# A larger VectorE share, half as many interleaved sets, and waits joined to operations, in a kernel that writes all products of the columns of a batch

## The chip, the cores and the metric

The kernel runs on one core of a Trainium2 chip. The time is the device time of that core in microseconds (us): the median of three runs for the kernel before. The profile is one execution recorded by the hardware profiler, whose span is a little shorter than the device time (1270.1 us against 1272.28 us for the same run).

Engines in the profile: DVE is VectorE, ACT is ScalarE, POOL is GpSimd, SP is SyncE, which here only issues transfers. A trailing q (DVEq, SPq) means the sequencer in front of an engine, which handles waits, counts and issues. Data leaves the core by 16 DMA engines that work side by side.

## The reference

```python
def reference(r_inputs):                       # r_inputs: (4096, 256), float32
    dot = jnp.einsum('bi,bj->bij', inputs, inputs)
    iu, ju = jnp.triu_indices(256)
    return dot[:, iu, ju]                      # (4096, 32896), float32
```

Each of the 4096 rows of 256 numbers becomes the 32,896 products of its upper triangle: x0\*x0, x0\*x1, ... x0\*x255, x1\*x1, and so on. The "triangle row" i of the output holds x_i times x_i ... x_255 and is 256 - i long. The input is 4.19 MB and the output 538.97 MB, so the kernel mostly writes.

## The kernel before

The 4096 batch rows lie as 128 partitions with 32 rows each. Two rows per partition (REPEAT = 2) make a *round*: 16 rounds in all. In each round the 32,896 output columns are cut into three *pieces* of 10,944, 10,976 and 10,976 columns, so there are 48 pieces. Two buffers (*places*) hold a piece each, in turn: while one is being written out by DMA, the other is filled.

A piece is filled by two engines. The front of its list of triangle rows goes to ScalarE (one operation for each triangle row and each of the two batch rows, a copy with a per-partition scale), the rest goes to VectorE (an elementwise multiplication which does both batch rows at once). `split` hands rows to ScalarE until what is left for VectorE fits a budget per element:

```python
BUDGETS = [0.85, 0.85, 0.85]
SETS = 4
PASS = 6        # pieces in one turn of the loop
AHEAD = 2
...
def vector_time(block):
    return sum(68 + 1.046 * REPEAT * n * m for (*_, n), m in vector_ops(block))

def split(block, budget):
    scalar, k = 0.0, 0
    while k < len(block):
        scalar += REPEAT * (184 + 0.837 * block[k][3])
        if vector_time(block[k:]) <= budget or scalar > vector_time(block[k + 1 :]):
            break
        k += 1
    return k                       # block[:k] to ScalarE, block[k:] to VectorE
```

One VectorE operation may take two neighbouring triangle rows (m = 2). The second row is one element shorter than the first, so such an operation writes one element too many, which falls on the first element of the next row, and the operation that writes that next row must come later. To leave time between the two, `interleave` cuts VectorE's list into SETS stretches and takes operations from each stretch in turn. An operation whose predecessor in its own stretch was a double one has to wait for a count on VectorE's own semaphore `v_own`:

```python
    def vector(h, pieces, ahead):
        done = 0
        for p in pieces:
            ...                    # every third piece: copy the new round's rows to xv
            if not ahead:
                take(nc.vector, free[p % PLACES], 16)   # wait until the place is written out
                nc.vector.sem_inc(go, 1)                # let ScalarE begin
            for _, _, _, block, lo in blocks(p, ahead):
                order = interleave(block)
                counted, waits = {len(order) - 1}, {}
                for k, (*_, before) in enumerate(order):
                    if before is not None and before > max(waits.values(), default=-1):
                        waits[k] = max(before, k - 2)
                        counted.add(waits[k])
                ...
                    if k in waits:
                        ins._wait_ge(v_own, number[waits[k]])
                    if k in counted:
                        ins.then_inc(v_own, 1)
                ...
                nc.vector.wait_ge(v_own, done).then_inc(v_done, 1)
```

`take` is a wait that also sets the count back. ScalarE's first operation of a piece waits for `go`. SyncE waits for `v_done` and `a_done` of a piece and then issues its transfer, which raises `free` of that place by 16 when all of it has landed:

```python
                if not ahead:
                    turns += 1
                    todo[0]._wait_ge(go, turns)                 # ScalarE
...
                take(nc.sync, v_done, 1)                        # SyncE
                take(nc.sync, a_done, 1)
                nc.sync.dma_start(...).then_inc(free[p % PLACES] if len(parts) == 1 else head, 16)
```

The first two pieces are filled before the loop (the first of them in five parts, so that transfers can begin early). The loop then has 8 turns; a turn fills four pieces (2, 3, 4, 5 of a group of six) and then, except in the last turn, pieces 0 and 1 of the next group:

```python
        with nc.Fori(0, passes, ...) as h:
            pieces_of(h, range(AHEAD, PASS), False)
            with engine.If(h < passes - 1):
                pieces_of(nc.s_assert_within(h + 1, 0, passes - 1), range(AHEAD), False)
```

Of the kernel before, what the change touches and what calls it, by code (L numbers as in the profile page):

```python
# [14 lines left out]
REPEAT = 2  # L15
PIECES = 3
PLACES = 2
SETS = 4
PASS = 6
AHEAD = 2  # L20


BUDGETS = [0.85, 0.85, 0.85]
FIRST = [512, 1536, 3584, 6400]


# [5 lines left out]
def runs(d: int, lo: int, hi: int) -> list:  # L32


    found, at = [], 0
    for i in range(d):
        a, b = max(at, lo), min(at + d - i, hi)
        if a < b:
            found.append((i, i + a - at, a, b - a))
        at += d - i  # L40
    return found


def vector_ops(block: list) -> list:

    ops, k = [], 0
    while k < len(block):  # L50
        i, j, at, n = block[k]
        m = 2 if k + 2 < len(block) and i == j else 1
        ops.append((block[k], m))
        k += m
    return ops


def interleave(block: list) -> list:


    sets, k = [], 0
    for left in range(SETS, 0, -1):
        share = -(-len(vector_ops(block[k:])) // left)
        end = k
        while end < len(block) and len(vector_ops(block[k : end + 1])) <= share:
            end += 1
        if left == 1:
            end = len(block)
        sets.append(vector_ops(block[k:end]))
        k = end  # L70
    order, last = [], {}
    for step in range(max(map(len, sets))):
        for s, ops in enumerate(sets):
            if step < len(ops):
                order.append((*ops[step], last.get(s)))
                last[s] = len(order) - 1 if ops[step][1] == 2 else None
    return order
# [6 lines left out]
def split(block: list, budget: float) -> int:  # L84
# [8 lines that stand above are left out]
    return k  # L93


def window(ap: bass.AP, free: list) -> bass.AP:
    return bass.AP(ap.tensor, ap.offset, [list(ap.ap[0]), *free])
# [3 lines left out]
def kernel(  # L101
# [14 lines left out]
    nc = tc.nc  # L116
# [4 lines left out]
    passes = groups // rounds  # L121
# [17 lines left out]
    def semaphore(name: str):  # L139
        return ctx.enter_context(nc.semaphore(name))  # L140

    free = [semaphore(f"free{k}") for k in range(PLACES)]
    head, v_done, a_done, go = (semaphore(s) for s in ("head", "v_done", "a_done", "go"))
# [3 lines left out]
    def take(engine, sem, value: int):  # L147
        engine.wait_ge(sem, value).then_inc(sem, -value)  # L148

    v_own, a_own = semaphore("v_own"), semaphore("a_own")  # L150

    def x_of(h, q: int) -> bass.AP:
        return xt[:, bass.ds(h, 1), q * each : (q + 1) * each].rearrange("p o d -> p (o d)")

    def blocks(p: int, ahead: bool):

        lo, hi = spans[p % PIECES]
        cuts = [lo, *(FIRST if ahead and p == 0 else []), hi]
        for a, b in zip(cuts, cuts[1:]):
            block = runs(d, a, b)  # L160
            k = split(block, 0.0 if ahead else BUDGETS[p % PIECES] * REPEAT * (b - a))
            yield a - lo, b - lo, block[:k], block[k:], lo

    def vector(h, pieces: range, ahead: bool):
        done = 0
        for p in pieces:
            place = places[p % PLACES]
            if p % PIECES == 0:
                ins = nc.vector.tensor_copy(xv[:, :each], x_of(h, p // PIECES))  # L169
                if done:  # L170
                    ins._wait_ge(v_own, done)
                ins.then_inc(v_own, 1)
                done += 1
                nc.vector.wait_ge(v_own, done)
            if not ahead:
                take(nc.vector, free[p % PLACES], 16)
                nc.vector.sem_inc(go, 1)  # L177
            for _, _, _, block, lo in blocks(p, ahead):
                order = interleave(block)

                counted, waits = {len(order) - 1}, {}
                for k, (*_, before) in enumerate(order):
                    if before is not None and before > max(waits.values(), default=-1):
                        waits[k] = max(before, k - 2)
                        counted.add(waits[k])
                number = {k: done + 1 + c for c, k in enumerate(sorted(counted))}
                for k, ((i, j, at, length), m, _) in enumerate(order):
                    at -= lo
                    ins = nc.vector.tensor_tensor(  # L189
                        place[:, :, at : at + m * length],  # L190
                        window(xv[:, j:], [[d, REPEAT], [1, m], [1, length]]),
                        window(xv[:, i:], [[d, REPEAT], [1, m], [0, length]]),
                        ALU.mult,
                    )
                    if k in waits:
                        ins._wait_ge(v_own, number[waits[k]])
                    if k in counted:
                        ins.then_inc(v_own, 1)
                done += len(counted)
                nc.vector.wait_ge(v_own, done).then_inc(v_done, 1)  # L200
        nc.vector.sem_inc(v_own, -done)  # L201

    def scalar(h, pieces: range, ahead: bool):
        done = turns = 0
# [42 lines left out]
                )  # L247

    def all_pieces(engine, pieces_of):
        pieces_of(0, range(AHEAD), True)  # L250
        if engine is not nc.sync:
            for sem in loaded[1:]:
                engine.wait_ge(sem, 16)
        kind = engine.engine
        with nc.Fori(
            0,
            passes,
            engines=OrderedEngineSet([kind]),
            head_slot={kind: 0} if engine is not nc.sync else {},
        ) as h:  # L260
            pieces_of(h, range(AHEAD, PASS), False)
            with engine.If(h < passes - 1):
                pieces_of(nc.s_assert_within(h + 1, 0, passes - 1), range(AHEAD), False)

    for (lo, hi), sem in zip(zip(loads, loads[1:]), loaded):
        nc.sync.dma_start(xt.rearrange("p h d -> p (h d)")[:, lo:hi], x_in[:, lo:hi]).then_inc(sem, 16)
# [6 lines left out]
    for engine, pieces_of in ((nc.vector, vector), (nc.scalar, scalar), (nc.sync, sync)):  # L273
        all_pieces(engine, pieces_of)
    for k in range(PLACES):
        take(nc.sync, free[k], 16)
    for sem in loaded:
        take(nc.sync, sem, 16)

# [26 lines left out]
```

## Time and profile before

| | before |
|---|---|
| median of 3 runs | 1272.26 us (1272.22 to 1272.28) |
| span of the profile | 1270.1 us |
| DVE busy | 896.2 us, 71%, 1733 instructions |
| ACT busy | 632.1 us, 50%, 1897 instructions |
| written to and read from HBM | 538.97 MB and 4.19 MB, 428 GB/s over the span |
| ACT idle before its piece, until DVE's sequencer raised `go` | 593.2 us, 46 times |
| DVE idle before its piece, until the place was free | 328.6 us, 46 times |

How to read it: "busy" counts the time in which an engine carries out an operation. An engine that is idle costs nothing unless something that sets the end waits for it. L189 is the line of VectorE's multiplication, L213 that of ScalarE's scaled copy, L148 the line of `take`, L177 the line that raises `go`, L245 the issue of a piece's transfer. "Landing" is the moment at which a transfer's last count has arrived.

### The profile page before, as it was taken

Reading aid. Unit: us, or ns where it says so; the run is one execution under the profiler, and the core shown is the slowest. Engines: PE = TensorE matmul, PEld = TensorE weight load, DVE = VectorE, ACT = ScalarE, POOL = GpSimd, SP = SyncE. Lnnn points to the kernel's source line nnn. Section 1 sums busy time; section 2 is a strip of 40 time slices with the busy share of each in tenths; the row PEclk is TensorE's granted clock in tenths of the full one; section 3 lists DMA queues with packets and bytes.
Section 4 is the critical chain, followed back from the end, with each engine's and each line's share of the span. In section 5 each row is a group of like instructions: output and inputs, shape, how many; then the busy total and the mean of one; then the engine's idle time right before and its main releaser. Section 6 shows DMA issues by size and latency. Waiting matters only on the chain. (4 is left out here: it accounts for less than half of the span.)

```text
span 1270.1 us, 4343 instructions
## 1 busy us (share of the span) xinstructions
DVE 896.2 (71%) x1733; ACT 632.1 (50%) x1897; POOL 0.2 (0%) x4
## 2 busy tenths in 40 slices
DVE  8867776777667776677757776677766777577760
ACT  8635635455364543645437453374534735257350
POOL 0000000000000000000000000000000000000000
DMA  9999999999999999999999999999999999999997
GB/s 380 437 440 426 437 440 422 441 422 440 422 441 421 440 423 439 430 432 439 424 437 424 439 423 440 422 440 425 437 428 433 422 442 420 441 421 441 421 420 336
DMA packets 14582, 543.22 MB, mean 428 GB/s; under 512 B 880, under 2 KB 880, under 8 KB 1520
## 3 DMA queue, kind: packets, MB, share of 16 engines
q1 hardware_dynamic: 14576, 543.17, 99.4%
q14 instruction: 6, 0.05, 0.0%
HBM read 4.19 MB, written 538.97 MB: 428 GB/s over the span
## 5 line engine op out<-in xcount | busy, mean ns | idle before, releaser
L189 DVE TENSOR_TENSOR o<-xv 128x752 f32<-128x752 f32 (+62 forms) x1716 | 889.3, 605 | 329.3 <-DVEq L148 328.6
L213 ACT ACTIVATE o<-xa 128x253 f32<-128x253 f32 (+58 forms) x1880 | 620.8, 423 | 593.4 <-DVEq L177 593.2
L169 DVE COPY xv<-x 128x512 f32 (+1 forms) x16 | 6.8, 427 | 9.0 <-DVEq L201 4.2
L208 ACT ACTIVATE xa<-x 128x512 f32 (+1 forms) x16 | 10.1, 630 | 5.6 <-ACTq L235 3.9
L208 ACT ACT_TABLE_LOAD x1 | 1.3, 1283 | 4.0 <-DMA x<-in_r_inputs_dram 4.0
L267 DVE MEMSET xv<- 128x1 f32 x1 | 0.1, 59 | 1.0 <-SPq L137 1.0
L293 POOL MEMSET const-bfloat16-1.0<- 128x1 bf16 x1 | 0.1, 102 | 0.0
L293 POOL MEMSET const-uint8-127<- 128x1 uint8 x1 | 0.1, 102 | 0.0
L293 POOL MEMSET const-float32-1.0<- 128x1 f32 x1 | 0.1, 99 | 0.0
L293 POOL MEMSET const-float32-0.0<- 128x1 f32 x1 | 0.1, 98 | 0.2 <-issue 0.2
## 6 DMA issues: line engine op xcount, KB each, us to landing
out_dram<-o SPq DMA_DIRECT2D x32, 10976.0 KB, 33.0
out_dram<-o SPq DMA_DIRECT2D x15, 10944.0 KB, 32.9
out_dram<-o SPq DMA_DIRECT2D x1, 4544.0 KB, 18.7
out_dram<-o SPq DMA_DIRECT2D x1, 2816.0 KB, 14.1
x<-in_r_inputs_dram SPq DMA_DIRECT2D x1, 2048.0 KB, 12.3
out_dram<-o SPq DMA_DIRECT2D x1, 2048.0 KB, 11.6
x<-in_r_inputs_dram SPq DMA_DIRECT2D x1, 1792.0 KB, 6.9
out_dram<-o SPq DMA_DIRECT2D x1, 1024.0 KB, 10.0
```

The source lines that it names most:

```text
L169: ins = nc.vector.tensor_copy(xv[:, :each], x_of(h, p // PIECES))
L189: ins = nc.vector.tensor_tensor(place[:, :, at : at + m * length], window(xv[:, j:], [[d, REPEAT], [1, m], [1, length]]), window(xv[:, i:] ...
L208: nc.scalar.activation(xa, x_of(h, p // PIECES), AF.Copy).then_inc(a_own, 1)
L213: nc.scalar.activation(place[:, r, at - lo : at - lo + length], xa[:, r * d + j : r * d + j + length], AF.Copy, scale=xa[:, r * d + i : r ...
L267: nc.vector.memset(xv[:, each:], 0.0)
L293: nc = _bacc.Bacc("TRN2", target_bir_lowering=False, num_devices=1)
```

## The change

The change does four things.

1. The budgets rise from 0.85 to 1.0, 1.0 and 0.95 ns per element of the three pieces of a round, so VectorE takes more triangle rows and ScalarE fewer: 74 ScalarE operations in a round in place of 116 (10, 16 and 48 in the three pieces, in place of 22, 32 and 62).
2. VectorE's list is interleaved from two stretches in place of four. It then has fewer operations for the same rows, because fewer pairs are cut at the borders of stretches, and each waiting operation comes two places behind the one that it waits for.
3. Waits and counts that stood as instructions of their own are joined to operations: the end of a piece raises `v_done` directly where `v_own` need not be told, and the count on `v_own` runs on from the four pieces into the next two.
4. A place's `free` count is no longer set back at each use. It runs to 16, 32, 48 over the three uses of a place in a group of six pieces. At the first two uses the wait for it raises `go` itself; at the third use (pieces 0 and 1 of the next group) the wait sets `free` back, and `go` is raised by a VectorE operation: the first of the piece that does not already raise `v_own`.

The purpose is to take instructions and ScalarE work out of the filling of a piece.

```diff
-SETS = 4
+SETS = 2
-BUDGETS = [0.85, 0.85, 0.85]
+BUDGETS = [1.0, 1.0, 0.95]
...
+    uses = PASS // PLACES
+    def use(p: int) -> int:
+        return (p - AHEAD) % PASS // PLACES + 1
...
             if not ahead:
-                take(nc.vector, free[p % PLACES], 16)
-                nc.vector.sem_inc(go, 1)
+                if use(p) < uses:
+                    nc.vector.wait_ge(free[p % PLACES], 16 * use(p)).then_inc(go, 1)
+                else:
+                    take(nc.vector, free[p % PLACES], 16 * uses)
...
-                counted, waits = {len(order) - 1}, {}
+                own = (p + 1) % PIECES == 0 or p == pieces[-1]
+                counted, waits = {len(order) - 1} if own else set(), {}
...
+                lets_go = -1
+                if not ahead and use(p) == uses:
+                    lets_go = next(k for k in range(len(order)) if k not in counted)
...
                     if k in counted:
                         ins.then_inc(v_own, 1)
+                    if k == lets_go:
+                        ins.then_inc(go, 1)
                 done += len(counted)
-                nc.vector.wait_ge(v_own, done).then_inc(v_done, 1)
-        nc.vector.sem_inc(v_own, -done)
+                if own:
+                    nc.vector.wait_ge(v_own, done).then_inc(v_done, 1)
+                else:
+                    ins.then_inc(v_done, 1)
+        return done
```

(The rest of the diff carries `done` through the loop and sets the counts back at its end.)

## The prediction

> **What bounds the kernel now.** I read the page's DMA part first, because the kernel mostly writes.
>
> ```profile
> DMA packets 14582, 543.22 MB, mean 428 GB/s; under 512 B 880, under 2 KB 880, under 8 KB 1520
> q1 hardware_dynamic: 14576, 543.17, 99.4%
> ```
>
> The transfer queue occupies the 16 DMA engines for 99.4% of the span, so the engines that fill the places are hidden at present. Whether they stay hidden depends on how early each transfer is issued, so next I took the timeline of three pieces in mid-run (columns: start, length, engine, line, operation, count, idle time before).
>
> ```profile
> 380.38 8.80 ACT L213 ACTIVATE o<-xa 128x256 f32<-128x256 f32 x22 [7.12 <-DVEq L177]
> 380.43 18.55 DVE L189 TENSOR_TENSOR o<-xv 128x980 f32<-128x980 f32 x20 [6.85 <-DVEq L148]
> 406.43 11.11 ACT L213 ACTIVATE o<-xa 128x7 f32<-128x7 f32 x32 [17.25 <-DVEq L177]
> 406.49 18.46 DVE L189 TENSOR_TENSOR o<-xv 128x776 f32<-128x776 f32 x26 [7.50 <-DVEq L148]
> 432.42 18.39 ACT L213 ACTIVATE o<-xa 128x98 f32<-128x98 f32 x62 [14.88 <-DVEq L177]
> 432.47 18.83 DVE L189 TENSOR_TENSOR o<-xv 128x468 f32<-128x468 f32 x61 [7.52 <-DVEq L148]
> ```
>
> A piece comes every 26.1 us (380.43 to 458.86, the next piece 0, is 78.43 for three). VectorE needs 18.5 to 18.8 us of it and then waits about 7 us for the other place. Its wait ends with a landing, so every piece starts at one.
>
> Last, the end of the run, in stretches (columns: window, length, busy DVE, ACT and POOL, clock, DMA share, GB/s).
>
> ```profile
> 1235.90:1236.40 0.50, 0.00 (x0) 0.00 (x0) 0.00 (x0) 1.00 0.00 0
> 1236.40:1236.90 0.50, 0.00 (x0) 0.00 (x0) 0.00 (x0) 1.00 2.29 966
> ...
> 1263.40:1265.00 1.60, 0.00 (x0) 0.00 (x0) 0.00 (x0) 1.00 0.06 27
> 1265.00:1266.60 1.60, 0.00 (x0) 0.00 (x0) 0.00 (x0) 1.00 0.06 27
> 1266.60:1268.20 1.60, 0.00 (x0) 0.00 (x0) 0.00 (x0) 1.00 0.06 27
> 1268.30:1270.00 1.70, 0.00 (x0) 0.00 (x0) 0.00 (x0) 1.00 0.00 0
> ```
>
> Two things are seen. The last transfer is issued at 1235.92 and the first packets after it start about 0.9 us later; the packet records put them at 1236.8 to 1237.0, so I use 0.95 us. And at the end one DMA engine alone works on (a share of 0.06, one sixteenth) for 5.3 us after the fifteen others are done. That slowest engine sets every landing and the end. In the landing records its lag grows from about 0.3 us at 328 us to 5 us at 1000 us and then stays, because the other fifteen then run dry for some tenths of a microsecond at each issue. The quantity that matters is therefore whether the *slowest* engine ever runs dry.
>
> **What the Trainium skill says.** "DMA: Bandwidth & Descriptors", section "Where 436 GB/s comes from", puts the ceiling of the 16 ports at 435 GB/s and says that the HBM side, about 358, binds such transfers. Here three pieces (33.69 MB) in 78.43 us are 430 GB/s, so the trace agrees with the first figure and not with the second. The same page, section "Latency and other measured facts", says that two of the engines, 7 and 15, are usually slower; the trace shows one slow engine, but not its number. "Perfetto Trace Analysis", section "DVE / Act Engine Instruction (TENSOR_ADD, Activation, etc)", says that an operation's count goes out only when all its bytes are acknowledged, at the end that the profile reports. The trace agrees: the count instruction that waits for a piece's last VectorE operation starts 39 ns after its end. Point three below rests on it. "VectorE: DVE Perf Modes", section "The DRAIN you can't avoid", measured that a count on every operation costs nothing extra; the trace agrees so far, as counted and waiting operations keep the same spacing as others.
>
> **The change part by part.** VectorE first. The kernel's own formula, 68 ns an operation and 1.046 ns an element, gives 18.51, 18.42 and 18.71 us for the 20, 26 and 61 operations before, against 18.55, 18.46 and 18.83 in the timeline, so I trust it. After the change the lists are 22 operations with 2 x 9694 elements (1.50 + 20.28 = 21.78 us), 29 with 2 x 9553 (1.97 + 19.99 = 21.96) and 63 with 2 x 7811 (4.28 + 16.34 = 20.63). In the third piece short operations (the last have a formula time of 72 to 150 ns) stand between an operation and the one it waits for, and I add up to 0.6 us there. So VectorE takes 21.8, 22.0 and about 21.1 us.
>
> How much would be harmless? For the slowest engine count from the landing that frees a place: 0.25 us until VectorE starts (landing at 380.18 in the records, start 380.43), the filling D, 0.4 us until the issue (372.91 to 373.30), 0.95 us until packets flow. The engine runs dry 26.1 us after that landing, less the 0.47 us which lie between a transfer's last packet and its landing (1268.30 and 1268.77): 25.65 us. So D may reach 24.05 us. All three VectorE times are below it. Of the four pieces 2 to 5 of a group nothing reaches the end; that part is worth 0 us. Joined counts save 0.1 to 0.2 us a piece, hidden likewise.
>
> Second, ScalarE's own time falls to 4.09 us (piece 0: its first ten operations, from 380.38) and 5.50 us (piece 1: its first sixteen). These are the same triangle rows as before, so the profile has them measured:
>
> ```profile
> 380.38 4.09 ACT L213 ACTIVATE o<-xa 128x256 f32<-128x256 f32 x10 [7.12 <-DVEq L177]
> ...
> 406.43 5.50 ACT L213 ACTIVATE o<-xa 128x7 f32<-128x7 f32 x16 [17.25 <-DVEq L177]
> ```
>
> Third, and this decides: at the third use of a place (pieces 0 and 1 of the next group) `go` is raised by the first VectorE operation that does not already raise `v_own`. With two stretches, each operation from the third on waits for the one two places before it, so almost all are counted. Worked through the lists: in piece 0, of 22 operations, numbers 0 to 19 are counted, so number 20 raises `go`; in piece 1, of 29, numbers 0 to 25 and the last are counted, so number 26 raises it. ScalarE, which before started with VectorE, starts there when VectorE has nearly finished.
>
> Piece 0: operation 20 starts 21.78 - 0.55 - 0.49 = 20.73 us in and takes 0.63 us (462 elements; the 128x460 operation before took 631 ns): 21.36. With 0.05 for the count and 4.09 for ScalarE, D is 25.5 us. Piece 1: 20.97 + 0.53 (352 elements) = 21.50, and with 0.05 and 5.50 it is 27.05 us.
>
> From landing to flowing packets: piece 0 takes 0.16 (no separate `go` any more) + 25.5 + 0.26 (ScalarE's count goes straight to SyncE) + 0.95 = 26.87 us against 25.65, so the slowest engine stands still for 1.2 us. Piece 1 takes 0.13 + 27.05 + 0.26 + 0.95 = 28.4 us. Its place came free with the transfer before piece 0's, and piece 0's transfer now ends 1.2 us late, so the allowance is 25.65 + 1.2 = 26.85 and it adds 1.5 us. The next piece has room again (its landing moved as well). That is 2.7 us a turn, in the seven turns that have the two pieces: 7 x 2.7 = 19 us. 1272.3 + 19 = 1291 us.
>
> The start and the end add nothing that I can see: the pieces before the loop keep their split, and the last turn has no third use.
>
> **Rivals.** (a) *Nothing moves*, 1272 us: the queue is 99.4% busy and VectorE's longer filling is inside its 7 us wait. This is right for pieces 2 to 5, and would hold for all if ScalarE's release came early. Against it stands the list of counted operations. (b) *VectorE becomes the bound*: if a wait on the operation two places back held each one by 0.1 us, D would grow by 2 to 3 us in pieces 0 and 1 and 6 us in piece 2; the stall would be 5 to 8 us a turn for pieces 0 and 1, and piece 2 would stall too, for 1310 us or more. Against it: 19 such waits in the third piece before left its total at 0.1 us over the formula. (c) *The slow DMA engine catches up.* All sixteen restart together in each turn. If its slowness, about 0.13 us a piece against the others, came from working while they rest, up to 5 us come back: 1286 us. (d) *Restarts cost more* than 0.95 us when all engines are dry: half a microsecond more, 14 times, makes 1298 us.
>
> **Range and chances.** The sum rests on two differences of about 1.2 and 1.5 us, each from terms good to 0.3 us, taken seven times: 4 us either way; (c) takes some off and (d) adds some. I choose 1284 to 1297 us. The 2% line is 1297.7 us, so slower by over 2% needs 3.6 us a turn in place of 2.7: a chance of 0.08. Faster by 2% would need less data to write: 0.01.
>
> **What would show it.** Right: in pieces 0 and 1 of six, ScalarE starts about 21.4 us after VectorE and waits for a VectorE operation, not for its sequencer; those issues come about 1.2 and 1.5 us after the slow engine ran dry; landings are 27.3 and 27.6 us apart there and 26.1 elsewhere. VectorE's pieces take 21.8, 22.0 and 21.1 us. Wrong: ScalarE starting with VectorE in all pieces (then rival a); VectorE's pieces over 24 us (rival b); stalls much over or under 2.7 us a turn.

## The result, and the profile after

| | before | after |
|---|---|---|
| median of four runs | 1272.26 us (1272.22 to 1272.28) | 1291.14 us (1291.06 to 1291.27) |
| ratio after to before | | 1.0148, 95% interval 1.0133 to 1.0163 |
| span of the profile | 1270.1 us | 1289.0 us |
| instructions in the profile | 4343 | 3720 |
| DVE busy | 896.2 us | 1030.1 us |
| ACT busy | 632.1 us | 413.1 us |
| DMA queue's share of 16 engines' span | 99.4% | 98.0% |

The change makes the kernel 18.9 us slower, 1.5%. The prediction was 1291 us, in a range of 1284 to 1297.

The page's DMA part after, to be held against the same two lines of before:

```profile
DMA packets 14582, 543.22 MB, mean 421 GB/s; under 512 B 880, under 2 KB 880, under 8 KB 1520
q1 hardware_dynamic: 14576, 543.17, 98.0%
```

Packets and bytes are the same. The share times the span is 0.994 x 1270.1 = 1262 us before and 0.980 x 1289.0 = 1263 us after, so the transfers themselves take as long as they did; what is new is time in which the queue has nothing to move.

The timeline of one turn of the loop shows where (start, length, engine, line, operation, count, idle time before and who ended it). The lines are pieces 0, 1 and 2, and then piece 0 of the next round, which is one of those with an early release:

```profile
465.00 21.80 DVE L202 TENSOR_TENSOR o<-xv 128x1004 f32<-128x1004 f32 x22 [4.57 <-DVEq L148]
486.34 4.08 ACT L231 ACTIVATE o<-xa 128x256 f32<-128x256 f32 x10 [32.13 <-DVE o L202]
491.05 21.98 DVE L202 TENSOR_TENSOR o<-xv 128x808 f32<-128x808 f32 x29 [4.26 <-DVEq L148]
512.52 19.95 ACT L231 ACTIVATE o<-xa 128x7 f32<-128x7 f32 x64 [22.10 <-DVE o L202]
518.15 20.89 DVE L202 TENSOR_TENSOR o<-xv 128x496 f32<-128x496 f32 x63 [5.11 <-DMA out_dram<-o]
...
545.92 4.08 ACT L231 ACTIVATE o<-xa 128x256 f32<-128x256 f32 x10 [12.62 <-DVEq L183]
545.98 21.80 DVE L202 TENSOR_TENSOR o<-xv 128x1004 f32<-128x1004 f32 x22 [6.27 <-DMA out_dram<-o]
```

In the first piece ScalarE starts 21.34 us after VectorE (486.34 and 465.00), in the second 21.47 us after it, each time released by a VectorE operation (`<-DVE o L202`). In the last two lines, an early release, the two engines start together. The x64 of the fourth line is the 16 operations of piece 1 and then the 48 of piece 2, without a gap.

The waits of the whole run (engine and line, waited for whom: us in total, times, longest) give the count: 14 late releases, two in each of seven turns.

```profile
ACT o L231 <- DVEq L183: 446.1, 26, 22.0
ACT o L231 <- DVE o L202: 379.6, 14, 32.2
```

Last, the DMA engines around those two pieces' transfers (window, length, busy DVE, ACT, POOL, clock, DMA share, GB/s):

```profile
490.40:491.50 1.10, 0.45 (x1) 0.02 (x1) 0.00 (x0) 1.00 0.00 0
491.50:492.00 0.50, 0.50 (x2) 0.00 (x0) 0.00 (x0) 1.00 3.29 1401
...
518.00:519.00 1.00, 0.85 (x2) 0.92 (x5) 0.00 (x0) 1.00 0.00 0
519.00:519.50 0.50, 0.50 (x2) 0.50 (x3) 0.00 (x0) 1.00 3.30 1405
```

These windows book a packet where it starts, which is why a share can exceed 1 and why a share of 0.00 alone does not show that the engines rest. The packet records give each packet's length as well: from 490.42 to 491.57 us and from 517.67 to 519.14 us no DMA engine has a packet. The whole run has 14 such gaps, two in each of seven turns, 18.3 us together; the loss is 18.9 us. In the kernel before, the packet records of the loop have no such gap: at least one engine, the slowest, always has work.

### The profile page after: what moved, and what is told of

Same layout as the page of the kernel before. It is cut to its first block, busy times and chain, and to the rows that moved or that the text cites. A ratio compares the mean times of both kernels' runs of the same rounds, so it can differ in the third digit from the quotient of the medians.

```text
span 1289.0 us, 3720 instructions
## 1 busy us (share of the span) xinstructions
DVE 1030.1 (80%) x1835; ACT 413.1 (32%) x1253; POOL 0.2 (0%) x4
## 5 line engine op out<-in xcount | busy, mean ns | idle before, releaser
L202 DVE TENSOR_TENSOR o<-xv 128x124 f32<-128x124 f32 (+61 forms) x1818 | 1023.2, 647 | 217.0 <-DMA out_dram<-o 148.0
L231 ACT ACTIVATE o<-xa 128x253 f32<-128x253 f32 (+38 forms) x1236 | 401.7, 416 | 826.4 <-DVEq L183 446.1
```

Of the source, the lines that this page charges most:

```text
L202: ins = nc.vector.tensor_tensor(place[:, :, at : at + m * length], window(xv[:, j:], [[d, REPEAT], [1, m], [1, length]]), window(xv[:, i:] ...
L231: nc.scalar.activation(place[:, r, at - lo : at - lo + length], xa[:, r * d + j : r * d + j + length], AF.Copy, scale=xa[:, r * d + i : r ...
```

## The experiments

The theory is that of the prediction: the late release of ScalarE makes two fillings a turn too long, and a filling costs nothing until it is so long that the slowest DMA engine stands still. (A *filling* here is the time from VectorE's first operation of a piece to the last operation of either engine.) The rivals are that VectorE's longer filling costs, that its waits on nearly every operation do, or that the two engines' working one after the other costs in proportion.

### The release early again, all else changed

```diff
+LATE = ()
...
                 else:
                     take(nc.vector, free[p % PLACES], 16 * uses)
+                    if p not in LATE:
+                        nc.vector.sem_inc(go, 1)
...
-                if not ahead and use(p) == uses:
+                if not ahead and use(p) == uses and p in LATE:
                     lets_go = next(k for k in range(len(order)) if k not in counted)
```

> Only the release of ScalarE at the third use of a place is put back to where it was before: ahead of VectorE's first operation. VectorE's share, the two stretches and all joined waits stay as in the changed kernel. Theory (the late release alone makes DMA engines run dry): the whole 18.9 us come back, 1272.3 us, within 1 us. Rival (VectorE's longer filling of 21 to 22 us costs, or waiting on nearly every operation does): 1291 us, or something between.

Measured: 1271.80 us, ratio 0.9996 (0.9988 to 1.0005). The whole loss is gone. The timeline of the same two pieces:

```profile
458.80 4.08 ACT L234 ACTIVATE o<-xa 128x256 f32<-128x256 f32 x10 [10.83 <-DVEq L188]
458.86 21.80 DVE L205 TENSOR_TENSOR o<-xv 128x1004 f32<-128x1004 f32 x22 [4.67 <-DVEq L149]
484.85 5.50 ACT L234 ACTIVATE o<-xa 128x7 f32<-128x7 f32 x16 [21.97 <-DVEq L188]
484.90 21.98 DVE L205 TENSOR_TENSOR o<-xv 128x808 f32<-128x808 f32 x29 [4.25 <-DVEq L149]
```

VectorE works as long as in the changed kernel (21.80 and 21.98 us), ScalarE begins with it, and a piece comes every 26 us again. VectorE's share, its two stretches and its waits cost nothing here.

The landing records show why longer fillings are free at first. The last transfer's slowest engine ends at 1268.66 us, against 1268.77 in the kernel before, but the fifteen others end by 1266.24 and not by 1263.32. With fillings of 22 us in place of 18.5 to 18.8 us, the fifteen end 3 us later, and the time does not move: the packet records still have no gap common to all engines, so the slowest one, which sets the end, still never stops.

### Four stretches, and the rule of the release untouched

```diff
-SETS = 2
+SETS = 4
```

> The changed kernel with four stretches in place of two, and nothing else. The rule that picks the releasing operation is untouched, but with four stretches the first operation of pieces 0 and 1 does not raise the count on VectorE's semaphore, so it now raises ScalarE's release: 1.1 to 1.3 us into the piece and not 21.4. Theory: 1272.3 us, within 1 us. Rival (joining the release to an operation costs in itself): 1291 us.

Measured: 1270.76 us, ratio 0.9988 (0.9981 to 0.9995). One constant, which does not mention the release, takes the loss away, because with four stretches the first operation of a piece is free to raise it:

```profile
458.37 21.86 DVE L202 TENSOR_TENSOR o<-xv 128x1004 f32<-128x1004 f32 x23 [4.60 <-DVEq L148]
459.61 4.08 ACT L231 ACTIVATE o<-xa 128x256 f32<-128x256 f32 x10 [11.96 <-DVE o L202]
```

ScalarE is again released by a VectorE operation, but 1.24 us into the piece. So joining the release to an operation costs nothing in itself; what costs is which operation it is. It is also the fastest kernel of this study, 0.12% ahead of the kernel before. I had expected 1272.3 us. Of the 1.5 us, 1.1 are spread over the whole run: from the landing at 172 us to the last one, the same 42 pieces take 1095.4 us here and 1096.6 us before (1096.4 with two stretches and an early release, the run above), so the slowest DMA engine itself is faster by about 0.03 us a piece. Why is open.

### A smaller VectorE share, with the late release

```diff
-BUDGETS = [1.0, 1.0, 0.95]
+BUDGETS = [0.85, 0.85, 0.85]
```

> The changed kernel with VectorE's budgets back at 0.85, so VectorE works less (18.5 us a piece) and ScalarE more (22, 32 and 62 operations). The release still comes at the 18th of 19 and the 23rd of 25 operations. Theory: pieces 0 and 1 of the next group take 18.0 + 8.8 = 26.8 us and 17.9 + 11.1 = 29.0 us; from landing to flowing packets that is 1.35 us more each, 2.5 us and then 2.2 us over the allowance, 4.7 us a turn, 7 turns: 33 us, so 1305 us (1301 to 1309), slower than the changed kernel. Rival (VectorE's larger share is the cost): 1272 us, as before.

Measured: 1305.48 us, ratio 1.0261 (1.0244 to 1.0278). Giving VectorE less makes the changed kernel 14 us slower still, as the late ScalarE then has more to do (the x94 of the last line is 32 operations of piece 1 and 62 of piece 2):

```profile
469.24 18.48 DVE L202 TENSOR_TENSOR o<-xv 128x980 f32<-128x980 f32 x19 [6.63 <-DVEq L148]
487.21 8.79 ACT L231 ACTIVATE o<-xa 128x256 f32<-128x256 f32 x22 [24.90 <-DVE o L202]
495.25 18.39 DVE L202 TENSOR_TENSOR o<-xv 128x776 f32<-128x776 f32 x25 [7.53 <-DVEq L148]
513.12 29.38 ACT L231 ACTIVATE o<-xa 128x7 f32<-128x7 f32 x94 [17.12 <-DVE o L202]
```

487.21 + 8.79 - 469.24 is 26.76 us of filling where 26.8 was expected. So once the release is late, VectorE's larger share, the part of the change that is named first, makes the loss smaller and not larger.

### Share and stretches alone, on the kernel before

```diff
-BUDGETS = [0.85, 0.85, 0.85]
+BUDGETS = [1.0, 1.0, 0.95]
-SETS = 4
+SETS = 2
```

> The kernel before with the new budgets and two stretches, and none of the joined waits: the release stands as an instruction of its own ahead of each piece. VectorE takes 21 to 22 us a piece, below the 24 us that I hold to be harmless. Theory: 1272.3 us, within 1 us. Rival (share and stretches cost by themselves): 1276 to 1291 us.

Measured: 1271.95 us, ratio 0.9998 (0.9989 to 1.0006): no difference.

### Late in one piece only

In piece 1 (first run) or piece 0 (second run) the release is early; in the other piece it is as late as in the changed kernel. For the first run, in VectorE's loop:

```diff
                     lets_go = next(k for k in range(len(order)) if k not in counted)
+                    if p == 1:
+                        lets_go = 0
...
+                    if p == 1 and lets_go == 0 and k == 1:
+                        nc.vector.wait_ge(v_own, number[0]).then_inc(go, 1)
-                    if k == lets_go:
+                    if p != 1 and k == lets_go:
                         ins.then_inc(go, 1)
```

For the second:

```diff
+LATE = (1,)
...
                     take(nc.vector, free[p % PLACES], 16 * uses)
+                    if p not in LATE:
+                        nc.vector.sem_inc(go, 1)
...
-                if not ahead and use(p) == uses:
+                if not ahead and use(p) == uses and p in LATE:
```

> The changed kernel, with the release late (operation 20 of 22) in piece 0 only; in piece 1 it comes after the first operation. Theory: 25.5 us of filling in piece 0, 1.2 us over the allowance, in seven turns: 8.3 us, so 1280.6 us (1278.5 to 1282.5). Rival (each late release costs the same share of the 18.9 us): 1281.7 us, not told apart by this run alone; together with the next run it is.

> The changed kernel, with the release late (operation 26 of 29) in piece 1 only; in piece 0 ScalarE starts with VectorE. Theory: nothing is delayed ahead of piece 1, so its 27.0 us of filling meet the full 25.65 us allowance and stand 2.7 us over it, in seven turns 19 us: 1291 us (1289 to 1293), the same as with both late. So the two lateness costs are not additive: 8 + 19 and not 27, but 19 together. Rival (the costs add): 18.9 - 8.3 = 10.6 us, 1283 us.

Measured: 1280.38 us with piece 0 alone late (ratio 1.0064, 1.0047 to 1.0081), 1290.76 us with piece 1 alone late (1.0146, 1.0129 to 1.0163). The costs are 8.1 and 18.5 us, and both together cost 18.9, not 26.6. Piece 1 is filled into the place that the transfer ahead of piece 0's left, so its filling starts on time even when piece 0 is late; but piece 0's late transfer also ends later, so the DMA engines run out of work later, and part of piece 1's lateness is covered. In the packet records, the gap in which no engine has a packet is 1.2 to 1.3 us in each turn with piece 0 alone and 2.7 to 2.9 us with piece 1 alone; with both late, the two gaps of a turn are about 1.2 and 1.4 us, 2.6 together. Mending piece 0 alone gains next to nothing: it is the second run, 1290.76 us against 1291.14.

### Where the cost begins

The release is raised by an instruction of its own that waits for a chosen VectorE operation: 16 and 20, then 18 and 23.

```diff
+RELEASE = {0: 16, 1: 20}        # then {0: 18, 1: 23}
...
-                    lets_go = next(k for k in range(len(order)) if k not in counted)
+                    lets_go = RELEASE[p]
+                    assert lets_go in counted
...
-                    if k == lets_go:
-                        ins.then_inc(go, 1)
+                    if lets_go >= 0 and k == lets_go + 1:
+                        nc.vector.wait_ge(v_own, number[lets_go]).then_inc(go, 1)
```

> The changed kernel, with the release after operation 16 in piece 0 and operation 20 in piece 1 (by an instruction of its own that waits for that operation). ScalarE still starts some 18 us after VectorE, but ends at 22.1 and 22.9 us, under the 24 us. Theory: no engine runs dry, 1272.3 us, within 1 us. Rival (what costs is that ScalarE and VectorE no longer work side by side, in proportion to the lateness): about 5/6 of the loss stays, 1287 us.

> As the last, with the release after operation 18 in piece 0 and 23 in piece 1: the fillings take 24.1 and 25.2 us. Theory: piece 0 just fits (0.2 us left), piece 1 is 0.9 us over, seven times: 6 us, 1278.3 us (1275 to 1281). Together with the other run this marks where the cost begins. Rival (proportional to lateness): about 1289 us.

Measured: 1271.90 us (ratio 0.9997, 0.9988 to 1.0006) and 1277.98 us (1.0045, 1.0028 to 1.0061). In the first of the two:

```profile
458.87 21.80 DVE L204 TENSOR_TENSOR o<-xv 128x1004 f32<-128x1004 f32 x22 [4.58 <-DVEq L149]
476.76 4.08 ACT L233 ACTIVATE o<-xa 128x256 f32<-128x256 f32 x10 [28.69 <-DVEq L215]
484.92 21.99 DVE L204 TENSOR_TENSOR o<-xv 128x808 f32<-128x808 f32 x29 [4.25 <-DVEq L149]
502.26 5.49 ACT L233 ACTIVATE o<-xa 128x7 f32<-128x7 f32 x16 [21.41 <-DVEq L215]
```

ScalarE starts 17.9 and 17.3 us late and it costs nothing, as the fillings end after 22.0 and 22.8 us. In the second run the filling of piece 0 takes 23.97 us (481.29 + 4.08 - 461.40) and that of piece 1 25.07 us:

```profile
487.47 21.99 DVE L204 TENSOR_TENSOR o<-xv 128x808 f32<-128x808 f32 x29 [4.27 <-DVEq L149]
507.05 5.49 ACT L233 ACTIVATE o<-xa 128x7 f32<-128x7 f32 x16 [21.67 <-DVEq L215]
```

Its packet records have one gap a turn, 0.84 to 0.88 us, always at piece 1's transfer and never at piece 0's. So the cost begins between 23.97 and 25.07 us. ScalarE's release 17.3 us into piece 1 costs nothing, and the release 21.5 us into it (piece 1 late alone) costs 18.5 us: there is a threshold, and the loss is not in proportion to the lateness.

### VectorE itself over the limit

```diff
-BUDGETS = [1.0, 1.0, 0.95]
+BUDGETS = [1.0, 1.0, 1.2]
```

with the early release of the first experiment.

> The changed kernel with the release early everywhere, and the third budget at 1.2: VectorE takes all but 12 ScalarE operations of piece 2, 72 operations and 26.5 us by the formula. Theory (any filling over about 24 us makes the slowest DMA engine run dry, whichever engine it waits for): 26.5 + 0.25 + 0.4 + 0.95 = 28.1 us against 25.65, 2.4 us over, 16 rounds, less one at the start: 36 us, so 1308 us (1303 to 1313). Rival (only the late release of ScalarE costs, VectorE's length never does): 1272 us.

Measured: 1309.25 us, ratio 1.0291 (1.0275 to 1.0306).

```profile
447.42 3.71 ACT L234 ACTIVATE o<-xa 128x98 f32<-128x98 f32 x12 [20.48 <-DVEq L184]
447.47 26.48 DVE L205 TENSOR_TENSOR o<-xv 128x568 f32<-128x568 f32 x72 [3.99 <-DMA out_dram<-o]
```

VectorE takes 26.48 us in piece 2 of every round, in which ScalarE's 12 operations are long over, and the kernel loses 37 us. The packet records have one gap in each of the 16 rounds: 4.0 us in the first and 2.2 to 2.5 us in the others. So it does not matter which engine is late. The first rival is right this far: VectorE's length does cost, but only beyond the same threshold.

### Which DMA engine is the slow one

These runs start from the kernel before and ask about its last 5.3 us, in which one engine works alone. The first tries to spare engine 15. Of the second piece, the last fifth of the columns goes out in two transfers, of 120 and of 8 partitions:

```diff
+RELIEF = 0.2
...
+                if ahead and len(parts) == 1:
+                    mid = hi - int((hi - lo) * RELIEF) // UNIT * UNIT
+                    for p0, p1, a, b in ((0, P, lo, mid), (0, 120, mid, hi), (120, P, mid, hi)):
+                        to = x_out[bass.ds(h, 1), p // PIECES, p0:p1, :, base + a : base + b]
+                        nc.sync.dma_start(
+                            to.rearrange("o p r c -> p (o r) c"), place[p0:p1, :, a:b]
+                        ).then_inc(head1, 16)
+                    continue
...
+    take(nc.gpsimd, head1, 48)
+    nc.gpsimd.sem_inc(free[1], 16)
```

> The kernel before, with one transfer cut in three: of the second piece, which is filled ahead of the loop, the first four fifths go out from 128 partitions, and the last fifth from partitions 0 to 119 and 120 to 127 in two transfers. The Trainium skill, DMA: Bandwidth & Descriptors, section Why a DMA increments its semaphore by 16 and not by 1, says that a transfer of this kind uses the largest number of engines up to 16 that divides the partitions, the lowest-numbered ones: 15 and 8 here, so engine 15 is spared a fifth of a piece, about 5.2 us. No byte is left out. Theory (one DMA engine, number 15, is slower than the others by 0.13 us a piece and sets the end by 5.3 us): the end comes 4 to 5 us earlier, 1267 to 1268.5 us. Rivals: the slow engine is another one, such as number 7, and it gets more instead: 1272 to 1273.5 us; or the lag follows whatever engine is last and nothing moves: 1272.3 us.

Measured: 1280.54 us, ratio 1.0065 (1.0052 to 1.0079), 8 us slower where 4 to 5 us faster was hoped for. The windows of that stretch (columns as above):

```profile
55.00:60.00 5.00, 5.00 (x18) 5.00 (x18) 0.00 (x0) 1.00 1.03 444
60.00:65.00 5.00, 2.48 (x12) 2.19 (x7) 0.00 (x0) 1.00 0.93 244
65.00:70.00 5.00, 0.00 (x0) 0.00 (x0) 0.00 (x0) 1.00 1.06 253
```

The engines are as busy as ever and move little more than half as much: in the packet records the 8,704-byte packets of the two odd transfers take 637 ns each (median), 14 GB/s an engine, against 1627 ns for the 43,904-byte ones, 27 GB/s. The size of the packets alone is not the reason: the 8,192-byte packets of an early output transfer of 128 partitions take 309 ns in the same run, 27 GB/s. What the reason is stays open. And nothing was spared. At the next landing (100.42 us) eight engines are 3 to 6 us ahead of the last one and eight within 2 us of it; the engine that then falls behind the others is last from there on, so it is among the late eight.

Two more runs tell where it is, with three small transfers more, of 7 and then of 8 partitions' input rows, to a scratch area:

```diff
+        if engine is nc.sync:
...
+            rows = xt.rearrange("p h d -> p (h d)")[0 : 4 * ENGINES : 4, :]     # ENGINES = 7, then 8
+            for k in range(3):
+                engine.dma_start(scratch[k, :ENGINES, :], rows).then_inc(extra, 16)
```

> The kernel before, with three small transfers more, right behind the second piece's: each writes the input rows of 7 partitions (32 KB each) to a scratch area. By the Trainium skill, DMA: Bandwidth & Descriptors, section Why a DMA increments its semaphore by 16 and not by 1, 7 rows use the lowest-numbered 7 engines, 0 to 6, and each gets three packets, some 3.6 us of work at the 27 GB/s that one engine shows. Theory (one slow engine sets the end, the others have 5 us to spare): nothing moves, 1272.3 us, if the slow engine is not among 0 to 6, and 1275.9 us if it is. Rival (the last one to finish is not always the same engine, the work as a whole sets the time): about 0.1 to 1.6 us more, whichever engines get it, here and in the next run alike.

> The same with 8 rows and so engines 0 to 7. Theory: if the slow engine is number 7, as the relieved kernel's slower end suggests together with the Trainium skill's remark (same page, section Latency and other measured facts) that 7 and 15 are usually slower, 1275.9 us here and 1272.3 in the other run. If it is one of 8 to 15, both runs stay at 1272.3; if one of 0 to 6, both give 1275.9.

Measured: 1276.48 us (ratio 1.0033, 1.0021 to 1.0045) and 1276.43 us (1.0033, 1.0021 to 1.0045). In the landing records of the piece that follows them, 7 engines are over 3 us behind the other 9 in the first run, and 8 behind 8 in the second, so the transfers did use as many engines as the Trainium skill says (DMA: Bandwidth & Descriptors, section Why a DMA increments its semaphore by 16 and not by 1). Both runs are 4.2 us longer: the landings end 3.7 and 3.6 us later, near the three packets' 3.6, and the rest lies after the last landing. One engine alone still works at the end of the first run:

```profile
1267.00:1272.00 5.00, 0.00 (x0) 0.00 (x0) 0.00 (x0) 1.00 0.06 26
```

The end alone does not tell which engine it is, as no run loads a set of engines that leaves the slow one out. The landing records do. In the first run the nine engines that were not loaded stay within 0.6 us of each other at every landing until the others have caught up with them, and none of them falls back. The engine that sets the end comes out of the seven: it is last at the landing after the three transfers (97.33 us), and from there it falls behind the six others as it does in the kernel before. If the seven are numbers 0 to 6, as the Trainium skill has it in the same section, it is neither 7 nor 15, which the page calls usually slower (section Latency and other measured facts; as a best guess, it puts that down to the descriptors of transfers issued by software, and the queue here is `hardware_dynamic`). No run here shows the numbers themselves, and why the engine is slow stays open.

## Why the prediction was right

**The late release was read from the lists, and it is what happens.** The prediction put it on operations 20 and 26; the profile has ScalarE 21.34 and 21.47 us after VectorE, where 21.4 and 21.5 were worked out, in exactly 14 pieces. Two runs take all of the loss away by moving the release alone (early; after operations 16 and 20), and a third by a constant that moves it along (four stretches).

**VectorE's times** were 21.80, 21.98 and 20.89 us, predicted as 21.8, 22.0 and about 21.1. The allowance of up to 0.6 us for short operations in the third piece was too wide: 20.89 is 0.26 us over the formula's 20.63.

**The limit of 24.05 us holds, and measures 24.2.** Fillings of 22.8 and 24.0 us leave no gap. In the four kernels where one late piece stands alone, the filling less the gap that follows it in the packet records is 24.2 us every time:

| run | filling | gap (median) | filling less gap |
|---|---|---|---|
| release at 23, piece 1 | 25.07 us | 0.86 us | 24.2 |
| late in piece 0 only | 25.42 us | 1.19 us | 24.2 |
| VectorE over the limit, piece 2 | 26.48 us | 2.26 us | 24.2 |
| late in piece 1 only | 26.96 us | 2.74 us | 24.2 |

So what a filling costs is its excess over this limit. The times agree: 1277.98, 1280.38, 1309.25 and 1290.76 us, and 1305.48 us with the smaller share, against 1278.3, 1280.6, 1308, 1291 and 1305 expected.

**The sum of 2.7 us a turn** is met: from the landing at 172 us to the last, the same 42 pieces take 1115.5 us after and 1096.6 us before by the landing records, 18.9 us in seven turns. Its two parts are met too, although the landings stand 27.1 and 27.8 us apart (490.92, 518.01, 545.81) and not 27.3 and 27.6. The prediction added its 1.2 and 1.5 us to one spacing of 26.1 for all pieces, but the same two transfers stand 26.0 and 26.3 us apart in the kernel before (484.68, 510.70, 537.00). Against those, the two spacings grow by 1.15 and 1.50 us, the mean of seven turns.

**Rival (a)**, nothing moves, holds wherever the release is early (1270.8 to 1272.0 us). **Rival (b)** fell: waits on nearly every operation leave VectorE's pieces at most 0.26 us over the formula. **Rival (c)** fell: between two restarts the slowest engine needs 26.12 us a piece (landings at 545.81 and 650.29, four pieces), against 26.14 before (327.85 and 1007.56, 26 pieces), so nothing is given back. **Rival (d)** fell too: in all 14 restarts the first packet starts 0.9 us after the issue (490.67 and 491.57, for one), although all engines had stopped.

## What to carry to other kernels

A kernel whose transfers are busy for 99% of the time has a fixed room for its fillings, here 24.2 us against 18.8 used, and each microsecond beyond it was lost: work out the latest moment at which the next transfer can be issued, from the slowest of the DMA engines, and hold every change to the filling against it. When a wait or a release is joined to an operation, look up *which* operation it lands on; a rule such as "the first that has no count yet" moves from the first to nearly the last when another constant changes. And two late steps in a row need not add up, so mend both before judging either.

## What the runs showed that I had not expected

- The slowest of the 16 DMA engines, which sets the end by about 5.3 us, is among the seven that a transfer of 7 partitions uses.
- A transfer of 120 partitions with 8.5 KB rows, beside one of 8 partitions, moved 14 GB/s an engine, half the rate of packets of nearly the same size in a transfer of 128 partitions, and cost 8 us for one fifth of one piece.
- The changed kernel with four stretches is faster than the kernel before, 1270.76 us (0.9988, 0.9981 to 0.9995), and 1.0 us faster than the same with two stretches and an early release, spread evenly over the run; the cause is open.
